# The last feed-forward layer in one written order, its last tile's cluster scores first, three tiles' bias on TensorE, and the last block's gate ahead of an out product

## The chip, the cores and the metric

One core of one Trainium2 chip (eight cores, of which the kernel uses one). The metric is device microseconds of one launch. A core has TensorE (PE; its weight loads are PEld), VectorE (DVE), ScalarE (ACT), GpSimd (POOL) and SyncE (SP), which issues most DMAs; each works through its own instructions in order, and engines wait for each other by semaphores.

## What is computed

Four residual layers over x, 4 sequences of 256 tokens with 512 channels, in f32:

```python
x = x + attention(layernorm(x))        # 32 heads, with an adapter prefix
x = x + ffn(layernorm(x))              # cluster-gated feed-forward
x = x + mixer(layernorm(x))            # state-space mixer: 8192 inner channels in 8 groups
x = x + ffn(layernorm(x))              # the same feed-forward weights again

def ffn(x):                            # x: 1024 tokens x 512
    dots = softmax(x @ centroids.T / 0.1)      # 64 clusters
    hits = dots > 0.01
    query_sel = any(hits, axis=1)              # a token is used if it hits any cluster
    cluster_sel = any(hits, axis=0)            # a cluster counts if any token hits it
    row_sel = cluster_sel[assignments]         # 512 outputs, each in a cluster
    return where(query_sel[:, None] & row_sel[None, :], x @ weight.T + bias, 0)

def mixer(x):
    proj = x @ in_proj_w.T             # gate (8192), xBC (conv of 4 taps, silu), dt
    y = ssd(...)                       # chunked scan with decays, + D * hs
    g = y * silu(gate)
    g = g / sqrt(mean of g*g over a group of 1024 channels + eps) * norm_w
    return g @ out_w.T
```

A column of `row_sel` depends on all tokens. So the last layer's result can be put into x only when the cluster scores of all tiles are there.

## The kernel before

**Tiles.** Tokens lie on the 128 partitions, in 8 tiles (TT = 8). The 512 channels are 4 pieces of 128 (KC = 4). Every f32 product is made of three matmuls on split operands, written by `mm3`: high x high (L115), high x low part of the weights (L116) and low x high (L117), for each of the pieces of the contraction. The high part is a rounding copy, made by ACT; the low part is a subtraction, made by DVE. Weights and activations are both split.

**Mixer.** The 8192 inner channels are 64 blocks of 128 (NB = 64), in 8 groups G of 8 (GB = 8). `block(i)` makes block i's x projection (24 matmuls `pp`), conv, the decays (`em`: ACT exponentials, DVE products) and the chunk products of block i-1 (`inner_products`, 64 matmuls `pyy`), and the gate projection of block i (24 matmuls `pp`, then ACT's silu, `gt`, in `gate`). `turn` transposes block i-1 (eight transposes `trx` in two PSUM tiles), `weigh` makes `xd` from them. Gated blocks `gb` are stored to DRAM (`spill`) and read again a token tile at a time (`recall`, tile `gr`, four blocks for one tile). Squares for the norm are summed in `sq` (`squared`), and summed over channels by `pqs` with `root` behind it.

**Out product.** `outer(q, t)` multiplies group q's `gh` (split `gr`) of token tile t with the split output weights `wo` into `pog`: two halves of 12 matmuls with 512 columns. It is done a group later, one tile in a block; `scaled` (L1237 on DVE) adds pog times the norm's factor to x. `upper_half` makes the high part (ACT, L1215) and leaves the low part (DVE, L1220) as a `lower` to be called later; `upper_out` does the same for output weights (L1174, L1177); `lowered()` calls all that are pending. The last group G-1 has no later group: its first halves are in `begin`/`begun`, and its second halves belong to the last feed-forward part. There the last of the eight pieces comes from a tile in SBUF (128 columns), and `gr` has only three pieces (384 columns). The chunk scores of the mixer (`scores`, matmuls `pg`, L1038, and DVE's `gm`, L1045) for the next group are made in the group's seventh block.

**Pools.** PSUM pool "m" has two slots, shared by `trx`, `pog` of `outer`, `pg`, `tr`; a matmul into it waits for the reader of the tile two before.

**Last feed-forward part.** For a tile: norm statistics (DVE, L138, L139), `root` (ACT Sqrt, L143), `scale` to gxn (DVE, L158), 4 transposes `tr` (PE), split into gxs (ACT L107, DVE L108), two halves of 12 matmuls with 288 columns into `pd` (64 cluster scores and 512 outputs together), then `chosen`: the row maximum (gnm), Exp on ACT (L218), hits, two bias adds (L229, L230) and one select-and-add (L231). After the last tile `select` counts hits over all tokens (cnt, msk), and eight times `take` (L243) copies the chosen columns into x, each with its output DMA.

**Order.** All blocks are under `manual_schedule`: the order on the engines is the program's. The last feed-forward part is not: a scheduler of the framework orders it, from costs and due times. ACT's Sqrt and Exp need different function tables, and a table load is put where the function changes.

Of the kernel before, what the change touches and what calls it, by code (L numbers as in the profile page):

```python
# [9 lines left out]
F32 = mybir.dt.float32  # L10
F32R = mybir.dt.float32r
# [3 lines left out]
AF = mybir.ActivationFunctionType  # L15
# [64 lines left out]
def hybrid_kernel(  # L80
# [29 lines left out]
    def mm3(o, ls, rs, first=True, last=True):  # L110

        n = len(ls)
        for k in range(n):
            (lh, ll), (rh, rl) = ls[k], rs[k]
            nc.tensor.matmul(o, lh, rh, start=(first and k == 0), stop=False)  # L115
            nc.tensor.matmul(o, lh, rl, start=False, stop=False)  # L116
            nc.tensor.matmul(o, ll, rh, start=False, stop=(last and k == n - 1))  # L117
# [57 lines left out]
    class Feed:  # L175


        def __init__(self, name, w1, p2):
            self.norm = Norm(name)
            self.name, self.p2 = name, p2  # L180
            t = lambda n, s, d=F32: w1.tile(s, d, name=f"{name}{n}")
            self.bias = t("b", [P, C])
            load(self.bias, ffb.to_broadcast([P, C]))
            idx = t("i", [NCL, 1])
            load(idx, cst[:NCL, COLS["idx"][0] : COLS["idx"][1]])
            asg_i = t("a", [NCL, C], I32)
            load(asg_i, asg.to_broadcast([NCL, C]))
            self.onehot = t("o", [NCL, C], BF16)
            nc.vector.tensor_scalar(self.onehot, asg_i, idx, None, ALU.is_equal)
            self.w = [t(f"w{j}", [P, KC, 2, FH], F32R) for j in range(2)]  # L190
            self.new = t("x", [P, TT, C])
            self.hits = t("h", [P, NCL])
            nc.gpsimd.memset(self.hits, 0.0)
# [9 lines left out]
                self.products(xs, j, halves[j])  # L203
            self.chosen(t, halves)

        def products(self, xs, j, o):
            mm3(o, [[v[:, k, :] for v in xs] for k in range(KC)],
                [[v[:, k, j, :] for v in self.w] for k in range(KC)])

        def chosen(self, t, halves):  # L210
            p2 = self.p2
            pa, pb = halves
            small = lambda n, w: p2.tile([P, w], F32, name=f"{self.name}{n}", tag=f"f{n}")
            nm = small("nm", 1)
            nc.vector.tensor_reduce(nm, pa[:, :NCL], AX.X, ALU.max, negate=True)
            nc.vector.tensor_scalar(nm, nm, 10.0, None, ALU.mult)
            e, se = small("e", NCL), small("se", 1)
            nc.scalar.activation(e, pa[:, :NCL], AF.Exp, bias=nm, scale=10.0, accum_out=se)  # L218
            nc.vector.reciprocal(se, se)
            hit, sel = small("hit", NCL), small("sel", 1)  # L220
            nc.vector.tensor_scalar(hit, e, se, 0.01, ALU.mult, ALU.is_gt)
            if t < TT - 1:
                nc.vector.tensor_tensor(self.hits, self.hits, hit, ALU.max)
            else:
                self.last = hit
            nc.vector.tensor_reduce(sel, hit, AX.X, ALU.max)
            new = self.new[:, t, :]
            m = FH - NCL
            nc.vector.tensor_tensor(new[:, :m], pa[:, NCL:], self.bias[:, :m], ALU.add)  # L229
            nc.vector.tensor_tensor(new[:, m:], pb, self.bias[:, m:], ALU.add)  # L230
            nc.vector.scalar_tensor_tensor(new, new, sel, x[:, t, :], ALU.mult, ALU.add)  # L231

        def select(self, cnt, rows):

# [551 lines left out]
    def mixer(feed, later):  # L786
        with ExitStack() as es, ExitStack() as inner:
# [504 lines left out]
                return q, t, po  # L1292

            xs2, gts, ems, xds, gbs = {}, {}, {}, {}, {}
            late_ = []

            def gate(i, pp):
                gts[i] = p2.tile([P, NT], F32, name="gt", tag="gt", bufs=2)
# [77 lines left out]
            def block(i):  # L1376
# [81 lines left out]
                        next(scoring)  # L1458

                next(g_steps)  # L1460
                if done or both:
                    inner_products(i - 1)
                    if both:
                        done = outer(G - 2, TT - 1)
                    pp = next(g_steps)
                    scored()
                    next(g_steps)
                else:
                    pp = next(g_steps)
                    scored()  # L1470
                    next(g_steps)
                    inner_products(i - 1)
                lower.append(upper_piece(n + 3))
                if g and gi == 0:
                    lower.append(upper_half(g - 1, 0))
# [5 lines left out]
                if both:  # L1481
                    for k in range(3):
                        fetch_out(NB - 3 + k)
                    begin(0)
                    lower.extend(upper_out(g * GB + k) for k in range(4))
                    scaled(*done)
                    lowered()
                    lower.extend(upper_out(g * GB + k) for k in range(5, GB))
                    begin(1)
                    lowered()  # L1490
                if scoring:
                    for _ in scoring:
                        pass
                if gi == 6:
                    for k in range(4):
                        fetch_out(g * GB + k)
# [7 lines left out]
                    group[NEXT[gi] + "pp"] = whole(projected(NEXT[gi], g + 1))  # L1504
                    upper_piece(n + 4)()

            pos, begins = {}, {}

            def begin(t):
                begins[t] = parts(G - 1, t, 0)  # L1510

            def begun(t):
                if t not in begins:
                    begin(t)
                pos[t] = ps_o.tile([P, C], F32, name="pog", tag="po")
                partial(pos[t], G - 1, begins.pop(t), 0)

            with tc.manual_schedule(
                engines={e.engine for e in (nc.tensor, nc.scalar, nc.vector, nc.gpsimd)}
            ):  # L1520
                opening()
                for i in range(2, NB):
                    block(i)
                es_p.close()
                ps_o = pool("m_o", 4, space=PSUM, **freed)
                i = NB - 1
                spilled(i - 1, gbs[i - 1])
                decays(i)
                turn(i)
                weigh(i)  # L1530
                begin(2)
                upper_out(i - 3)()
                wos[G - 1].insert(4, wos[G - 1].pop())
                for t in range(3):
                    begun(t)
                begin(3)
                squared(i - 1, xs2.pop(i - 1), gbs.pop(i - 1))
                inner_products(i)
                spilled(i, gbs[i])
                begun(3)  # L1540
                partial(pos[0], G - 1, parts(G - 1, 0, 1), 1)
                squared(i, xs2.pop(i), gbs.pop(i))
                rgs[G - 1] = root(sums(G - 1))
                nc.vector.reciprocal(rgs[G - 1], rgs[G - 1])
            es_y.close()
            inner.close()
            ps_d = pool("f_d", 2, space=PSUM, side="right", **freed)
            f1, f2 = pool("f1", 1, **freed), pool("f2", 2, **freed)
            feed = Feed("g", f1, f2)
            for k in range(KC):  # L1550
                feed.weights(k)
            ov = out.rearrange("(t p) c -> p t c", p=P)
            turned_ = {}

            def fed(t):
                where = (ps_o, "po") if t == TT - 1 else (ps_d, "pd")
                feed.tile(
                    t, turned_.pop(t), [where[0].tile([P, FH], F32, name="pd", tag=where[1]) for _ in range(2)]
                )

            for t in range(TT):
                po = pos.pop(t)
                if t:
                    partial(po, G - 1, parts(G - 1, t, 1), 1)
                scaled(G - 1, t, po)
                if t + 4 < TT:
                    begun(t + 4)
                feed.norm.stats(t)
                rooted = feed.norm.root(t, t + 1)

                with tc.issue_after(rooted) if t == TT - 1 else ExitStack():
                    for n in range(*{TT - 2: (0, 0), TT - 1: (t - 2, t)}.get(t, (max(0, t - 1), t))):
                        fed(n)
                xn = f2.tile([P, C], F32, name="gxn", tag="gxn")
                tr = ps.tile([P, KC, P], F32, name="tr", tag="m")
                turned_[t] = [f2.tile([P, KC, P], F32R, name=f"gxs{j}", tag=f"gxs{j}", bufs=3) for j in range(2)]
                feed.norm.turned(t, xn, tr, turned_[t])
            primed(AF.Exp)
            fed(TT - 1)
            feed.select(ps.tile([NCL, P], F32, name="cnt", tag="m"), ps.tile([P, C], F32, name="msk", tag="m"))  # L1580
            for t in range(TT):
                feed.take(t)
                load(ov[:, t, :], x[:, t, :])

    later = ExitStack()
    mixer(attention(later), later)
# [69 lines left out]
```

## Time and profile before

| | us |
|---|---|
| runs: median (lowest, highest), 3 runs | 1847.87 (1845.71, 1849.84) |
| the profiled execution: time | 1849.91 |
| its span, first to last instruction | 1848.1 |
| mean granted TensorE clock in the span | 0.986 |
| PE busy | 1777.1 |
| DVE busy | 1425.8 |
| ACT busy | 1276.9 |

The span runs from the first to the last instruction; the launch's time is 1.8 us longer than the span in this execution. Times in the text are us from the span's start. "Idle before" in a group's row is the time in which the engine did nothing before these instructions, with what ended it. The granted clock is 1.00 at full speed and 0.50 at half. In the part concerned: the last gate projection 1742.0 to 1747.4, the first products of the last group's tiles from 1748.4, pog(1,1) from 1774.6, first `pd` finished at 1787.1, last `pd` at 1837.0, takes 1838.9 to 1843.9, end 1848.1.

### The profile page before, as it was taken

The page shows a single profiled execution, that of the slowest core. Times are in us where ns is not written, and L with a number is a line of the kernel's source. Part 1 is how long each engine was busy: PE and PEld are TensorE (multiplying, and loading weights), DVE is VectorE, ACT ScalarE, POOL GpSimd, SP SyncE. Part 2 cuts the span into 40 slices and gives each one's busy share as a digit, 9 for nine tenths or more (in the row PEclk, how much of TensorE's full clock was granted, in tenths as well). Part 3 has the DMA queues.
Part 4 walks back from the last instruction along what each step waited for, and adds up shares of the span by engine and source line. Part 5 has one row for each costly group of instructions (what it writes and reads, how often), then busy time and mean ns, then how long its engine had stood idle before and what let it go on. Part 6 is the DMA issues. An engine that isn't in the chain of part 4 may idle for free.

```text
span 1848.1 us, 33082 instructions
## 1 busy us (share of the span) xinstructions
PE 1777.1 (96%) x12882; PEld 1448.5 (78%) x12882; DVE 1425.8 (77%) x2155; ACT 1276.9 (69%) x2520; POOL 245.0 (13%) x251
## 2 busy tenths in 40 slices
PE   7999989899999999999999999999999999999997
PEld 6777767677777888888888888888888888888776
DVE  5566667678989787878887787879787878887766
ACT  6666676367778667866776686668667866767743
POOL 6322330000110111001101110110111011101100
PEclk9999999999999999999999999999999999999999
DMA  4000000112325323432442343224333532343231
GB/s 146 1 1 1 23 15 2 47 59 86 103 86 160 107 95 111 140 104 92 125 135 78 106 162 99 98 86 160 92 104 97 160 104 92 110 137 114 92 88 50
DMA packets 134238, 169.45 MB, mean 92 GB/s; under 512 B 12225, under 2 KB 77377, under 8 KB 134081
## 3 DMA queue, kind: packets, MB, share of 16 engines
q1 hardware_dynamic: 125008, 134.30, 23.9%
q10 hardware_dynamic: 9072, 33.03, 4.7%
q8 instruction: 101, 1.65, 0.4%
q14 instruction: 57, 0.46, 0.1%
HBM read 131.64 MB, written 35.65 MB: 91 GB/s over the span
## 4 chain that ended last, share of the span: by engine, by line
PE 80%; DVE 8%; ACT 7%; issue 2%; POOL 2%; DMA 1%; SPq 0%; ACTq 0%; DVEq 0%; POOLq 0%
PE pp L115 13%; PE pp L116 13%; PE pp L117 13%; PE pyy L1120 7%; PE pog L115 6%; PE pog L117 6%; PE pog L116 6%; PE trx L1101 3%; ACT e L477 2%; PE ptr L493 1%; DVE acc L1008 1%; PE pq L115 1%; ACT em L1081 1%; PE pg L1038 1%; PE pq L116 1%
## 5 line engine op out<-in xcount | busy, mean ns | idle before, releaser
L115 PE MATMUL pp<-mx,w 128*128 128x512 f32 (+1 forms) x1160 | 463.6, 400 | 5.7 <-DVE acc L1008 5.1
L117 PE MATMUL pp<-mx,w 128*128 128x512 f32 (+1 forms) x1160 | 452.0, 390 | 0.0
L116 PE MATMUL pp<-mx,w 128*128 128x512 f32 (+1 forms) x1160 | 451.5, 389 | 0.0
L1153 POOL TENSOR_TENSOR sq<-sq,x 128x1024 f32<-128x1024 f32 x54 | 129.9, 2406 | 1205.0 <-ACT x L1152 1205.0
L115 PEld LDWEIGHTS pp<-mx,w 128*128 128x128 f32 x1160 | 218.3, 188 | 51.5 <-issue 5.5
L117 PEld LDWEIGHTS pp<-mx,w 128*128 128x128 f32 x1160 | 218.3, 188 | 46.3 <-DVE w L830 0.7
L116 PEld LDWEIGHTS pp<-mx,w 128*128 128x128 f32 x1160 | 218.7, 189 | 40.6
L1008 DVE SCALAR_TENSOR_TENSOR acc<-pp,cw_s,acc 128x1012 f32<-128x1012 f32 (+2 forms) x192 | 244.7, 1274 | 6.1 <-ACT acc L997 1.5
L1094 DVE TENSOR_TENSOR em<-em,gm 128x1280 f32<-128x1280 f32 x128 | 189.5, 1489 | 74.4 <-ACT em L1089 74.4
L115 PE MATMUL pog<-wo,gh 128*128 128x512 f32 x512 | 201.7, 394 | 3.4 <-ACT gh L1215 3.4
L117 PE MATMUL pog<-wo,gh 128*128 128x512 f32 x512 | 200.7, 392 | 1.0 <-DVE gh L1220 1.0
L116 PE MATMUL pog<-wo,gh 128*128 128x512 f32 x512 | 200.4, 391 | 0.0
L1104 DVE TENSOR_TENSOR xd<-trx,dt_t 128x512 f32<-128x512 f32 x128 | 82.4, 686 | 151.3 <-PE trx L1101 151.3
L1020 ACT ACT_TABLE_LOAD x63 | 80.8, 1283 | 154.6 <-DVE acc L1008 154.5
L1299 ACT ACTIVATE gt<-pp 128x1024 f32<-128x1024 f32 x64 | 65.6, 1026 | 156.5 <-PE pp L117 156.4
L1120 PEld LDWEIGHTS pyy<-em,xd 64*64 64x64 f32 x4096 | 129.5, 134 | 44.6 <-issue 18.4
L1081 ACT ACTIVATE em<-r,end_t 128x128 f32<-128x128 f32 x512 | 163.0, 389 | 0.8
L1120 PE MATMUL pyy<-em,xd 64*64 64x256 f32 (+3 forms) x4096 | 157.6, 302 | 2.4 <-DVE em L1094 2.4
L477 ACT ACTIVATE e<-sc,nmx 128x256 f32<-128x256 f32 (+1 forms) x256 | 104.2, 442 | 21.0 <-DVE nmx L471 20.9
L115 PEld LDWEIGHTS pog<-wo,gh 128*128 128x128 f32 x512 | 96.5, 189 | 23.6 <-ACT gh L1215 3.9
L117 PEld LDWEIGHTS pog<-wo,gh 128*128 128x128 f32 x512 | 96.6, 189 | 22.3 <-DVE gh L1220 2.2
L116 PEld LDWEIGHTS pog<-wo,gh 128*128 128x128 f32 x512 | 96.7, 189 | 19.5
(293 smaller groups left out, 3180.5 us busy)
## 6 DMA issues: line engine op xcount, KB each, us to landing
wr<-in_win_dram SPq DMA_DIRECT2D x144, 256.0 KB, 2.7
r<-cumd SPq DMA_DIRECT2D x256, 128.0 KB, 2.9
spill<-gb ACTq DMA_DIRECT2D x63, 512.0 KB, 3.2
gr<-spill SPq DMA_DIRECT2D x120, 256.0 KB, 3.5
wor<-in_wout_dram SPq DMA_DIRECT2D x64, 256.0 KB, 4.4
out_dram<-x SPq DMA_DIRECT2D x8, 256.0 KB, 2.5
x<-in_x_dram SPq DMA_DIRECT2D x1, 1536.0 KB, 8.8
gr<-spill SPq DMA_DIRECT2D x8, 192.0 KB, 2.5
```

The lines of the kernel that those rows point to most:

```text
L115: nc.tensor.matmul(o, lh, rh, start=(first and k == 0), stop=False)
L116: nc.tensor.matmul(o, lh, rl, start=False, stop=False)
L117: nc.tensor.matmul(o, ll, rh, start=False, stop=(last and k == n - 1))
L477: nc.scalar.activation(es_[c][:, 2 * j + pr, :], sc[:, j, :], AF.Exp, bias=nm[:, j : j + 1], accum_out=rs[:, c, h : h + 1],)
L1008: nc.vector.scalar_tensor_tensor(av[:, :, d:], pv[:, :, : L - d], cw_s[:, ch, tap : tap + 1], av[:, :, d:], ALU.mult, ALU.add,)
L1020: nc.scalar.activation(pair(x2).rearrange("p k u i -> p u k i"), acc.rearrange("p (u k i) -> p u k i", u=2, i=Q), AF.Silu,)
L1081: nc.scalar.activation(piece(e, j, c, 2 - c, 2), rv[:, j, 2:, :], AF.Exp, bias=end_t[:, 2 * j + c, h : h + 1],)
L1094: nc.vector.tensor_tensor(e, e, gm, ALU.mult)
L1104: nc.vector.tensor_tensor(xd[:, hs, :].rearrange("p c (h d) -> p c h d", h=2), tr.rearrange("p c (h d) -> p c h d", h=2), dt_t[:, hs, 2 * ...
L1120: nc.tensor.matmul(py[d, u, j * L + c * Q : (j + 1) * L].rearrange("p (k i) -> p k i", i=Q), xd[us, 4 * j + c, d], piece(es2[hh], j, c)[us ...
L1153: (nc.gpsimd if n < NB - 2 else nc.vector).tensor_tensor(sqs[g], sqs[g], x2, ALU.add)
L1299: nc.scalar.activation(gts[i], pp, AF.Silu)
```

## The change

1. In `Feed`, the bias tile gets 64 zero columns in front (a POOL memset in each of the two feed-forward layers), so that it lies as the products do. `products` can take a range of columns, and can begin its group with one plain f32 matmul of the identity with the bias. `chosen` becomes a generator, `choice`, with the hits before the outputs; where `biased`, the two bias adds and the select become two select-and-adds straight from PSUM. The last layer does this for tiles 5, 6 and 7.
2. In block 63, the gate projection goes ahead of `inner_products(62)` and of out product (6, 7). The recalls, output-weight pieces and lowers around them are in a new order, with `scaled` behind the pending lowers, and the output-weight pieces 5 to 7 after the decays.
3. In block 6 of group 0 the steps 1 and 2 of the next group's `scores` go after both halves of the gate, and the other two wait for block 7.
4. The last feed-forward part comes under `manual_schedule`, in a written order: in a loop for t = 2 to 6, second half of pog(t), x(t), statistics, recall and high parts for t+3 and t+1, root, Exp table, transposes of t-1, products and choice of t-2, Sqrt table, the lowers that are left, and the first half of pog(t+3). `primed(...)` loads a table ahead by an activation of one column.
5. At the end, tile 7's 64 cluster columns are computed before its other columns, the count and mask before its second half, and seven takes before tile 7's select.

The order on ACT in one turn of the loop before and after the change is different: after it, root, Exp table load, gxs, Exp, Sqrt table load, then the high parts of the next turn. On DVE the lower of gh(t+1,1) stands behind `choice(t-2)` for t = 2, 3, 4.

```diff
@@ Feed
-            self.bias = t("b", [P, C])
+            self.bias0 = t("b", [P, NCL + C])
+            self.bias = self.bias0[:, NCL:]
+            nc.gpsimd.memset(self.bias0[:, :NCL], 0.0)
...
-        def products(self, xs, j, o):
-            mm3(o, [[v[:, k, :] for v in xs] for k in range(KC)],
-                [[v[:, k, j, :] for v in self.w] for k in range(KC)])
+        def products(self, xs, j, o, cols=slice(0, FH), biased=False):
+            if biased:
+                nc.tensor.matmul(
+                    o[:, cols], ident, self.bias0[:, FH * j + cols.start : FH * j + cols.stop],
+                    start=True, stop=False,
+                )
+            mm3(o[:, cols], [[v[:, k, :] for v in xs] for k in range(KC)],
+                [[v[:, k, j, cols] for v in self.w] for k in range(KC)], not biased)
...
-            nc.vector.tensor_tensor(new[:, :m], pa[:, NCL:], self.bias[:, :m], ALU.add)
-            nc.vector.tensor_tensor(new[:, m:], pb, self.bias[:, m:], ALU.add)
-            nc.vector.scalar_tensor_tensor(new, new, sel, x[:, t, :], ALU.mult, ALU.add)
+            for part, cs in ((pa[:, NCL:], slice(0, m)), (pb, slice(m, C))):
+                if biased:
+                    nc.vector.scalar_tensor_tensor(
+                        new[:, cs], part, sel, x[:, t, cs], ALU.mult, ALU.add
+                    )
+                else:
+                    nc.vector.tensor_tensor(new[:, cs], part, self.bias[:, cs], ALU.add)
+                yield
+            if not biased:
+                nc.vector.scalar_tensor_tensor(new, new, sel, x[:, t, :], ALU.mult, ALU.add)
...
@@ block
                 next(g_steps)
-                if done or both:
+                for _ in pending:
+                    for _ in pending.pop():
+                        pass
+                if done and not both:
                     inner_products(i - 1)
-                    if both:
-                        done = outer(G - 2, TT - 1)
                     pp = next(g_steps)
                     scored()
                     next(g_steps)
                 else:
                     pp = next(g_steps)
+                    next(g_steps)
                     scored()
-                    next(g_steps)
                     inner_products(i - 1)
+                if both:
+                    done = outer(G - 2, TT - 1)
...
                 if both:
...
-                    begin(0)
+                    lower.append(made(0, 0))
                     lower.extend(upper_out(g * GB + k) for k in range(4))
+                    lower.append(made(1, 0))
+                    lowered()
                     scaled(*done)
-                    lowered()
-                    lower.extend(upper_out(g * GB + k) for k in range(5, GB))
-                    begin(1)
-                    lowered()
-                if scoring:
+                if scoring and g:
                     for _ in scoring:
                         pass
+                elif scoring:
+                    pending.append(scoring)
...
@@ after the blocks
                 decays(i)
                 turn(i)
                 weigh(i)
-                begin(2)
-                upper_out(i - 3)()
+                multiplied(0, 0)
+                multiplied(1, 0)
+                lower = [upper_out(i + k - 7) for k in (5, 6, 7)]
+                lower.append(made(2, 0))
+                lower.append(upper_out(i - 3))
...
+                settled(0)
+                normal(0)
+                multiplied(1, 1)
+                lower = made(4, 0)
+                settled(1)
+                lower()
+                multiplied(4, 0)
+                normal(1)
...
+                for t in range(2, TT - 1):
+                    multiplied(t, 1)
+                    settled(t)
+                    lower = [made(t + 3, 0)] if t + 3 < TT else []
+                    lower.append(made(t + 1, 1))
+                    lower.pop(0)()
+                    normal(t)
+                    lower.append(turned_(t - 1))
+                    for j in range(2):
+                        product_half(t - 2, j)
+                    lower.pop()()
+                    for _ in choice(t - 2):
+                        pass
+                    primed(AF.Sqrt)
+                    for f in lower:
+                        f()
+                    if t + 3 < TT:
+                        multiplied(t + 3, 0)
...
+                product_half(t, 0, slice(NCL, FH))
+                feed.select(cnt, ps.tile([P, C], F32, name="msk", tag="m"))
+                product_half(t, 1)
+                for _ in c6:
+                    pass
+                for t in range(TT - 1):
+                    feed.take(t)
+                    load(ov[:, t, :], x[:, t, :])
+                for _ in c7:
+                    pass
+                feed.take(TT - 1)
+                load(ov[:, TT - 1, :], x[:, TT - 1, :])
```

Here `made(t, half)` recalls gh(t, half), makes its high part and returns its lower; `multiplied(t, half)` is the 12 matmuls of that half of pog(t); `settled(t)` is `scaled` and the statistics; `normal(t)` is root, the Exp table and gxn; `turned_(t)` is the transposes and the high part of gxs, and returns its lower; `product_half(t, j, cols)` is half j of `pd`.

## The prediction

> **What bounds the kernel now.** I read the busy shares and the chain first, then the windows of the last 114 us, TensorE's waits there, and last the groups that give durations.
>
> ```profile
> PE 1777.1 (96%) x12882; PEld 1448.5 (78%) x12882; DVE 1425.8 (77%) x2155; ACT 1276.9 (69%) x2520; POOL 245.0 (13%) x251
> PE 80%; DVE 8%; ACT 7%; issue 2%; POOL 2%; DMA 1%; SPq 0%; ACTq 0%; DVEq 0%; POOLq 0%
> ```
>
> TensorE is the bound nearly everywhere: an order can only remove its few holes, or make new ones. The windows of the end (span start to 1848.1; busy us of PE, PEld, DVE, ACT, POOL, then clock, DMA share, GB/s):
>
> ```profile
> 1742.00:1748.00 6.00, 6.00 (x30) 4.97 (x29) 6.00 (x11) 3.59 (x7) 0.15 (x1) 1.00 0.33 100
> 1754.00:1757.00 3.00, 0.96 (x3) 0.40 (x2) 1.83 (x2) 2.97 (x7) 0.00 (x0) 0.89 0.00 0
> 1757.00:1765.00 8.00, 7.50 (x75) 5.25 (x74) 3.15 (x5) 2.35 (x4) 0.00 (x0) 0.62 0.63 176
> 1804.00:1814.00 10.00, 10.00 (x64) 9.16 (x64) 7.59 (x25) 6.43 (x13) 0.00 (x0) 1.00 0.00 1
> 1825.00:1831.00 6.00, 4.64 (x34) 4.07 (x33) 4.60 (x16) 3.48 (x8) 0.00 (x0) 1.00 0.00 0
> 1837.00:1848.00 11.00, 1.30 (x6) 0.47 (x5) 6.83 (x15) 0.00 (x0) 0.00 (x0) 0.71 0.52 191
> ```
>
> Two holes: 2.0 us in 1754 to 1757 (2.2 from end to start in the timeline) with half clock behind it (0.62, and in the timeline from 1756.3 to 1763.15), and 1.8 us at 1828 to 1830. The feed-forward loop between (1804 to 1814) is dense: a tile's first product starts 9.28 us after the last one's (1787.29, 1796.54, 1805.82).
>
> ```profile
> PE pog L115 <- ACT gh L1215: 3.4, 2, 2.0
> PE tr L166 <- DVE gxn L158: 1.2, 1, 1.2
> PE pog L117 <- DVE gh L1220: 1.0, 2, 0.5
> ```
>
> The durations that I use (mean ns after "busy us"):
>
> ```profile
> L231 DVE SCALAR_TENSOR_TENSOR gx<-gx,gsel,x 128x512 f32<-128x512 f32 x8 | 6.0, 746 | 0.1
> L108 DVE TENSOR_TENSOR gxs<-tr,gxs 128x512 fp32r<-128x512 f32 x7 | 4.8, 687 | 2.9 <-ACT gxs L107 2.9
> L230 DVE TENSOR_TENSOR gx<-pd,gb 128x288 f32<-128x288 f32 x8 | 3.6, 456 | 4.5 <-PE pd L117 4.5
> L229 DVE TENSOR_TENSOR gx<-pd,gb 128x224 f32<-128x224 f32 x8 | 3.0, 372 | 0.0
> L1220 DVE TENSOR_TENSOR gh<-gr,gh 128x384 fp32r<-128x384 f32 x5 | 2.7, 548 | 1.2 <-PE pd L117 1.2
> L218 ACT ACT_TABLE_LOAD x6 | 7.7, 1283 | 2.4 <-DVE gnm L216 2.3
> ```
>
> In the timeline, successive matmuls start 0.227 us apart for 512 columns (12 of a half tile: 2.73) and 0.1325 for 288 (24 of `pd`: 3.18); a tile's 4 transposes take 0.44. So a feed tile's TensorE work is 2 x 2.73 + 3.18 + 0.44 = 9.07 of the 9.28.
>
> **A. Blocks 6 and 7 of group 0 (scores later): -1.0.** Before, `pg` waits 1.6 us and block 7's `trx` 1.7 us for DVE's gm (waits, 510 to 545). With steps 3 and 4 in block 7 both go. But block 7's `gb` is also held by ACT's exponentials and DVE's products, which start only 0.95 earlier: gain 1.0, ends 0 and 2.7.
>
> **B. Block 63 to the start of pog(1,1): -5.1.** The gate's 24 matmuls go ahead of `pyy`(62) and of the 24 of pog(6,7); nothing is saved in work, but ACT's gate can start at 1746.2 (it waited until 1747.85 before) and the exponentials (5.34 us from table load to last) end with it. New order on PE from 1734.27: gate 5.45, pyy(62) 2.34 and pog(6,7) 5.45 to 1747.51, first four transposes 0.44. Then a new wait: block 63's second four need a PSUM slot that is freed by DVE's `scaled` (L1237), and this now stands behind three gb operations 2.58, four differences 1.87, a gh lower 0.60, four output-weight lowers 2.64, another lower 0.60: from 1742.2 DVE reaches and ends it at 1751.2. PE stalls 3.3 us. After that pog(0,0) and (1,0) to 1757.14, when DVE's second weigh (1755.44) is past: pyy(63) starts at once where it waited before, to 1759.48 at full clock; three more pog (8.18) to 1767.66 and pqs 1.84 to 1769.5. Before it was 1774.62.
>
> **C. Clock: +2.0.** The row for 1757 to 1765 shows what a hole costs here: 2.2 us of idle, then 6.8 us at half clock. The 3.3-us stall is longer, so I expect the same: half clock for about 3.4 us at least, hence +1.7, up to 3.4 if a second stretch follows[...]. [...] I keep +2.0 (ends 0 and 3.4).
>
> **D. First feed-forward part: +4.8.** ACT now has a written order: root(0), the Exp table load with its priming, and only then the hi cast of gh(4,0). From pqs at 1769.5: root 0.35, reciprocal 0.2, x(0), statistics, aggregate 1.6, root 0.3, load and priming 1.5: the cast starts at 1774.0 and ends at 1774.55. PE has done pog(1,1) at 1772.2 and stalls 2.4, then 0.3 for the lower. pog(2,1) then waits for its cast behind Sqrt load, root(1), Exp load and two casts of the feed weights (0.85), and for the DVE lower (1.55). Together 5.1 of stalls; before had about 0.3 of that stretch. SP's loads move too: the recall of gr(1,1) goes ahead of the bias and weight loads, gr(4,0) and gr(2,1) come between weights. They land in 2.5 to 3.6 us, ahead of their casts, so I cost the queue at nothing; if that cover went, a landing would be added to D. POOL's memset of the 64 columns is one more like the 0.15-us one of `hits`; POOL is idle there: nothing.
>
> **E. Loop t = 2, 3, 4: +4.6.** The lower part of gh(t+1,1) (L1220, 128x384) now stands on DVE behind all of `choice(t-2)`, and pog(t+1,1)'s third matmul needs it. So a ring closes, from one such lower to the next: the rest of pog(t,1) 2.4; x, statistics, aggregate 1.6; root 0.31; Exp load 1.3 and priming 0.2; gxs hi on ACT 0.6 and lower on DVE 0.62; the two gnm 0.40; exponential 0.55; reciprocal, ghit, hits, gsel 0.65; two bias adds and L231 1.45; the lower 0.55; some 0.2 of hand-overs. Sum 10.8, against 9.28: +1.5 per tile, three times. Before, the scheduler had the lower ahead of these. DVE is busy only some 7.0 of the 10.8: it is not throughput but order. [...] In the trace an exponential starts 1.30 us after its load started (1811.70, 1813.00)[...].
>
> **F. t = 5 to the end: +2.8.** For tiles 5, 6, 7 the two bias adds (0.46 + 0.37 per tile) leave DVE; a plain-f32 identity matmul enters PE six times. No row has one of this size: `pa` (L421, plain f32, 256 columns) takes 0.427 each in pitch[...], so 288 columns are an estimated 0.48 and 224 0.37: 5 x 0.48 + 0.37 = 2.77. Ends: 0.8[...] and 3.3. Tile 7's 64 columns by themselves: 12 at no less than 0.11 (the one-column steps of pqs) plus 12 x 224 columns at some 0.105, against 12 x 0.1325: +1.0 (ends 0.3 and 1.5). pog(7,1) stands behind pd(4), so x(7) comes at 15.9 us after the start of pog(5,1), not 13.3, and its transposes stall 1.6. Against it tile 7's other columns (1.6 + 1.6) go behind the count. Counted: cnt 26.6 after that start (before 25.2), msk 27.7, first take 28.65, seven takes to 32.9, tile 7's select and take to 34.75, then the output's 4.2 (as from 1843.86 to 1848.1): 39.0 against 36.24.
>
> **Sum.** -1.0 - 5.1 + 2.0 + 4.8 + 4.6 + 2.8 = +8.1. The profiled execution took 1849.91 (span 1848.1 and 1.8 around it), 2.0 over the median. So the span would be 1856.2, and against the median 1847.87 + 8.1 = **1856.0**.
>
> **Rivals.** (1) The forecast, about 0.56: the order closes the ring of E and the stalls of D. (2) More half clock, 0.18: [...] two or three more stretches of 1.7 to 3.4: about 1862. (3) No change, 0.14: D is half of what I count (ACT gets to gh(4,0) before its priming matters) and E +2: 1847.9 - 1 - 5.1 + 2 + 2.4 + 2 + 2 = 1850. (4) Faster, 0.12, by one mechanism: the lower of gh(t+1,1) lands before its matmul. TensorE reaches that at 9.1 + 0.43 after pog(t,1)'s start; if it is there, the ring never binds. It needs DVE and ACT to do the tile 1.5 us faster than my row-by-row sum, in D as well as E, from which A and B stay whole: 1847.9 - 6.1 + 0 to 1 of F = about 1842. For it: DVE and ACT have 20 to 30% idle in the loop. Against: the idle is waits for each other, in a chain. (5) Also under (3) and (4): that the change doesn't do what its words say. The bias on TensorE loads the engine that is the bound; it helps only where DVE is last. The row of L230 shows DVE idle for 4.5 us before those adds, for TensorE's `pd`: there it is TensorE that is last.
>
> **How the numbers follow.** The measurement can tell about 0.2% (3.7 us) from no change: 1844.2 to 1851.6. Faster is case 4, 0.12; same is case 3, 0.14; slower is cases 1 and 2, 0.74. The range runs from 1848.5, leaving out case 4 and a little of case 3, to 1863.5, leaving out the upper third of case 2: with the unknown ends of C and F (+1.4 and +1, or -2 and -2.7) inside.
>
> **What would show it.** Right: PE idle of about 3 us on `trx` of block 63 with DVE's `scaled` (x, L1237 as of before) as releaser; clock under 1 shortly behind it; pyy(63) without a wait; PE waits for ACT gh (2.4) and three times 1.3 to 1.9 for DVE gh of 128x384; starts of pog(t,1) 10.6 to 11 us apart; pd from gb at 0.45 to 0.5 each; last take some 4 us before the end. Wrong: starts still 9.3 apart (E), no ACT gh wait (D), no hole at trx (B, C), or the time from pog(5,1) to the end at or under 36.

## The result, and the profile after

The changed kernel takes 1855.95 us (median of 6 runs, 1851.77 to 1857.8) against 1848.86 (6 runs); the ratio is 1.0039, with a 95% interval of 1.0023 to 1.0056. It is slower, by about 7.1 us; forecast were 1856.0 and +8.1.

The page's busy line and the shares of its chain, for the kernel after (span 1855.7):

```profile
PE 1780.4 (96%) x12906; PEld 1452.3 (78%) x12906; DVE 1426.9 (77%) x2152; ACT 1286.0 (69%) x2536; POOL 245.3 (13%) x253
PE 78%; DVE 9%; ACT 8%; issue 2%; POOL 1%; DMA 1%; SPq 0%; ACTq 0%; DVEq 0%; POOLq 0%
```

TensorE's busy time is up by 3.3 us and the span by 7.6. So more than half of the loss is idle time of TensorE, and in the chain PE has 78% of the span where it had 80%, and DVE and ACT have 1% more each. The waits of TensorE from 1734 us on say where (line, releaser, us in total, times, longest):

```profile
PE pog L117 <- DVE gh L1245: 6.0, 5, 2.1
PE trx L1126 <- DVE x L1262: 3.1, 1, 3.1
PE pog L115 <- ACT gh L1240: 2.8, 2, 2.0
PE tr L1610 <- DVE gxn L158: 1.2, 1, 1.2
PE msk L264 <- DVE gc L263: 0.4, 1, 0.4
```

In the mixer the lines of after are 25 higher than those of before; L1245 is the gh lower, L1262 is `scaled`. Before, the DVE gh wait was 1.0 and there was no `trx` wait. The windows of the end (columns as above):

```profile
1748.00:1754.00 6.00, 2.94 (x15) 2.52 (x16) 5.85 (x9) 5.92 (x16) 0.15 (x1) 1.00 0.44 131
1754.00:1757.00 3.00, 3.00 (x15) 2.30 (x13) 3.00 (x4) 3.00 (x6) 0.00 (x0) 1.00 0.02 5
1757.00:1765.00 8.00, 8.00 (x89) 6.60 (x89) 7.40 (x11) 3.82 (x8) 0.00 (x0) 1.00 0.43 136
1794.00:1804.00 10.00, 9.57 (x48) 8.09 (x46) 6.25 (x18) 5.38 (x11) 0.00 (x0) 0.83 0.14 43
1814.00:1825.00 11.00, 9.52 (x57) 8.48 (x58) 6.45 (x19) 4.70 (x10) 0.00 (x0) 1.00 0.06 18
```

The hole is at 1748 to 1754 now (2.94 of 6.00 busy), and the row for 1757 to 1765, which had 0.62 before, is at full clock: the 3.1-us stall brought no half clock in this execution. A stretch at 0.83 turns up in the feed-forward loop instead.

Stages between the same instructions compare the executions better than times from the start. Block 4's silu starts anywhere from 481.0 to 488.7 us in the eleven profiles, though all that the change puts ahead of it is a memset on POOL, while the stretch from block 20's silu to block 61's takes 884.04 or 884.05 in every one. From starts in the timelines:

| stage | forecast | before | after | change |
|---|---|---|---|---|
| A: silu of block 4 to silu of block 9 | -1.0 | 89.53 | 88.62 | -0.9 |
| B: silu of block 61 to pog(1,1) | -5.1 | 71.81 | 66.89 | -4.9 |
| C: half clock behind the `trx` stall | +2.0 | (in B) | none | 0 |
| D: pog(1,1) to the second tile's transposes, less the pd that lies in it before | +4.8 | 9.33 | 14.02 | +4.7 |
| E: three turns of the loop (before: 3 x 9.28) | +4.6 | 27.84 | 34.44 | +6.6 |
| F: the rest of the span | +2.8 | | | +1.5 |

With 0.7 from the part ahead of block 4 these make the 7.6 of the span, to rounding. In A the waits of 1.6 and 1.7 us for DVE's gm are gone; TensorE's waits between 510 and 560 us sum to 2.8 instead of 4.4.

The ring of E, in the timeline of after (start, us, engine, line, operation; one turn, from statistics to lower):

```profile
1797.78 0.30 ACT L143 ACTIVATE grs<-gmv,eps 128x1 f32<-128x1 f32 x1 [1.91 <-DVE gmv L139]
1798.09 1.28 ACT L127 ACT_TABLE_LOAD   x1
1799.39 0.20 ACT L127 ACTIVATE primed<-ones 128x1 f32<-128x1 f32 x1
1799.50 0.57 ACT L1611 CAST gxs<-tr 128x512 fp32r<-128x512 f32 x1
1800.10 0.69 DVE L1612 TENSOR_TENSOR gxs<-tr,gxs 128x512 fp32r<-128x512 f32 x1 [0.92 <-ACT gxs L1611]
1801.20 0.32 ACT L233 ACTIVATE ge<-pd,gnm 128x64 f32<-128x64 f32 x1 [1.14 <-DVE gnm L231]
...
1801.65 0.16 DVE L235 RECIPROCAL gse<-gse 128x1 f32<-128x1 f32 x1 [0.54 <-ACT ge L233]
1803.19 0.75 DVE L255 SCALAR_TENSOR_TENSOR gx<-gx,gsel,x 128x512 f32<-128x512 f32 x1
1803.86 0.55 DVE L1245 TENSOR_TENSOR gh<-gr,gh 128x384 fp32r<-128x384 f32 x1
...
1804.46 0.50 PE L117 MATMUL pog<-wo,gh 128*128 128x512 f32 x1 [0.89 <-DVE gh L1245]
```

Each engine waits for another in turn. The lower ends at 1804.41, and at 1804.46 TensorE starts the third matmul of pog(4,1), which closes the ring. The starts of that matmul are 11.5, 11.9 and 11.0 us apart.

### The profile page after: what moved, and what is told of

Its sections match the earlier page's. It is cut to its first block, busy times and chain, and to the rows that moved or that the text cites. A ratio compares the mean times of both kernels' runs of the same rounds, so it can differ in the third digit from the quotient of the medians.

```text
span 1855.7 us, 33140 instructions
## 1 busy us (share of the span) xinstructions
PE 1780.4 (96%) x12906; PEld 1452.3 (78%) x12906; DVE 1426.9 (77%) x2152; ACT 1286.0 (69%) x2536; POOL 245.3 (13%) x253
## 4 chain that ended last, share of the span: by engine, by line
PE 78%; DVE 9%; ACT 8%; issue 2%; POOL 1%; DMA 1%; SPq 0%; ACTq 0%; DVEq 0%; POOLq 0%
PE pp L115 13%; PE pp L116 12%; PE pp L117 12%; PE pyy L1145 7%; PE pog L117 6%; PE pog L115 6%; PE pog L116 6%; PE trx L1126 3%; ACT e L502 2%; DVE acc L1033 1%; PE ptr L518 1%; PE pq L115 1%; ACT em L1106 1%; PE pg L1063 1%; PE pq L116 1%
```

## The experiments

**1. The lower out of the ring.**

```diff
@@ loop for t, kernel after
                     lower.pop(0)()
                     normal(t)
-                    lower.append(turned_(t - 1))
+                    for f in lower:
+                        f()
+                    lower = turned_(t - 1)
...
-                    for f in lower:
-                        f()
```

> The kernel after, with one edit: in the loop for t = 2 to 6 the lower of gh(t+1,1) stands on DVE right behind gxn(t), ahead of gxs and of choice(t-2). Theory (ring through choice): starts of the tiles' products fall from 11.0-11.9 us apart to about 9.3, the three DVE gh waits inside the loop (1.5 to 2.1 us each) vanish, and the time falls by 5 to 6.5 us, to about 1850 (ratio to before about 1.000). Rival (DVE or ACT throughput sets the pace, not order): starts stay 10.5 or more apart, the waits move to another releaser, under 1.5 us gained.

Measured: 1849.53 us (14 runs), ratio to before 1.0004 (0.9994 to 1.0014). The turns take 9.08 us each, TensorE's own work and nothing else. The window of three turns:

```profile
1784.00:1811.00 27.00, 27.00 (x156) 23.96 (x155) 19.97 (x54) 16.45 (x33) 0.00 (x0) 1.00 0.17 49
```

27.00 of 27.00 us busy, with DVE at 74%. One place in DVE's order was worth 6.4 us in the medians; throughput was not the bound of the loop.

**2. `scaled` ahead of the lowers in block 63.**

```diff
-                    lowered()
                     scaled(*done)
+                    lowered()
```

> The kernel after, with one edit: in block 63 DVE's scaled of out product (6,7) stands ahead of the pending lowers instead of behind them. Theory (the second four transposes wait for this instruction): their stall falls from 3.1 to about 0.9 us; but pyy(63) then waits for the decays' products at about 1755.5, so only 1.5 to 2 of the 2.2 reach pog(1,1), and the time falls by about 1.7 us. Rival (ACT's exponentials or the lowers themselves bind): the stall moves to pog(0,0) or to pyy(63) whole, and pog(1,1) starts within 0.5 us of where it did (1769.5).

Measured: 1855.79 us, as after (ratio to before 1.0037, 1.0023 to 1.0051). TensorE's waits, those that changed:

```profile
PE pog L117 <- DVE gh L1245: 7.0, 6, 2.2
PE pyy L1145 <- DVE em L1119: 0.5, 1, 0.5
PE trx L1126 <- DVE x L1262: 0.4, 1, 0.4
PE pog L116 <- DVE wo L1202: 0.4, 1, 0.4
```

The stall at `trx` fell from 3.1 to 0.4, more than I expected. But of these 2.7 us pog(0,0) lost 0.7 behind the lowers, pyy(63) 1.1 behind the decays and the products after it 0.5: from block 61's silu to pqs it is 64.78 us against 65.19. My 1.7 was wrong and the rival right, that the stall moves on. The window of this stretch:

```profile
1749.00:1758.00 9.00, 7.84 (x36) 5.45 (x34) 8.58 (x12) 8.92 (x20) 0.15 (x1) 1.00 0.29 89
```

DVE and ACT are both busy nearly throughout (8.58 and 8.92 of 9.00 us). Which of the two binds was not tried apart.

**3. The bias of tiles 5 to 7 back on DVE.**

```diff
-                BIASED = (5, 6, 7)
+                BIASED = ()
```

> The kernel after, with the bias of tiles 5, 6 and 7 added on DVE again, none by TensorE. Theory (the bias matmuls cost TensorE about 0.4 to 0.48 each on the path that sets the end; DVE has room before the count): the count comes 1.5 to 2.4 us earlier, but DVE's select of tiles 6 and 7 costs 0.6 more each behind it, so 0.5 to 1.5 us are gained. Rival (what the change was made for: DVE binds at the end): DVE's 1.9 us more are on the path, and the time rises by 1 to 2 us.

Measured: 1857.64 us, ratio to before 1.0051 (1.0035 to 1.0068), an interval that overlaps with that of after: unclear. In its profile the transposes of tile 7 wait 2.2 us instead of 1.2, for without bias matmuls TensorE arrives earlier; behind them TensorE runs at half clock, and from those transposes to the count it takes 9.82 us instead of 8.08. Half clock stands behind the `trx` stall too, where after has none. So this run could not tell the bias from the clock, and I repeated it without the ring (7).

**4. The blocks' part alone, the tail as before.** The blocks are those of after up to the square of block 63; from there on stands the text of before.

```diff
@@ kernel after, from the last squared() on
-                lower = made(1, 1)
...
-                settled(0)
-                normal(0)
...
+            for t in range(TT):
+                po = pos.pop(t)
+                if t:
+                    partial(po, G - 1, parts(G - 1, t, 1), 1)
+                scaled(G - 1, t, po)
+                if t + 4 < TT:
+                    begun(t + 4)
...
```

> The change's blocks alone (scores of group 0 later, gate of block 63 first, its lowers and the first products of the last group in the new order), with the last feed-forward part left to the scheduler as before, bias on DVE. Theory (the front is a gain of 5, which the written order of the tail gives back): pog(1,1) starts about 5 us earlier than before (1769.5 against 1774.6), the tail's 73 us are as before, and the time falls by 4 to 5 us to about 1844 (ratio 0.997 to 0.998). Rival (the front's gain is taken up by the tail's first waits, whatever its order: casts of recalled tiles and weights come no earlier): pog(1,1) starts earlier, but the first pd block and the end do not, under 1.5 us gained.

Measured: 1843.52 us (20 runs), ratio to before 0.9977 (0.9969 to 0.9985): 4.9 us faster in the medians, and faster than both kernels. Waits from 1730 us on:

```profile
PE trx L1126 <- DVE x L1262: 3.1, 1, 3.1
PE tr L166 <- DVE gxn L158: 1.0, 1, 1.0
PE pog L115 <- DVE x L1262: 0.4, 1, 0.4
PE msk L264 <- DVE gc L263: 0.4, 1, 0.4
```

None is of gh: with the scheduler's order the tail takes the front's gain to the end. So the tail of after (its order, its bias matmuls and the split of tile 7 together) costs what the front gives, and 7 more.

**5. Casts ahead of root and table, 6. no Exp priming before the loop.**

```diff
@@ on top of experiment 1
                 settled(0)
+                made(4, 0)()
                 normal(0)
                 multiplied(1, 1)
-                lower = made(4, 0)
+                lower = made(2, 1)
                 settled(1)
                 lower()
...
-                lower = made(2, 1)
                 turned_(0)()
-                lower()
@@ experiment 6, besides
-                    primed(AF.Exp)
+                    if t > 1:
+                        primed(AF.Exp)
```

> The kernel with the early lower (e1_lower_early), and in the first feed-forward part the recall of gh(4,0), its high part and its lower ahead of root(0), those of gh(2,1) ahead of the second tile's statistics and of the feed weights' casts. Theory (the 5 us of stalls before the loop come from ACT's written order: root and Exp table load ahead of a cast): the ACT gh wait of 2.0 us and the DVE gh waits of 1.4 us go, and from pog(1,1)'s start to the second tile's transposes it takes 9.5 to 10.5 us instead of 14.0; the time falls by 3.5 to 4.3 from e1's 1849.5, to about 1845.5. Rival (the recalls' DMAs or the feed weights land no earlier): PE waits for gr by way of ACT gh at another place, or the first pd block waits for gw; under 1.5 us gained.

> e5_casts_first without the Exp priming of tiles 0 and 1, which no Exp uses: two Exp and two Sqrt loads of 1.28 us less on ACT before the loop. Theory: after e5 ACT has still 5 us of useless loads there, ahead of the feed weights' casts; if pd(0) waits for those in e5, it starts earlier and 0.5 to 2 us more are gained; if it doesn't, nothing. [...]

Measured: 5 takes 1850.48 us, ratio 1.0014 (1.0001 to 1.0027), no gain on experiment 1; 6 takes 1848.67, ratio 0.9991 (0.9979 to 1.0004). In 5 the waits for ACT gh are gone, as expected, but others came:

```profile
PE pd L115 <- ACT gw L107: 1.4, 1, 1.4
PE pog L117 <- DVE gh L1245: 0.8, 1, 0.8
PE pd L117 <- DVE gxs L1612: 0.5, 1, 0.5
PE pd L116 <- DVE gw L108: 0.4, 1, 0.4
```

The first `pd` now waits for the feed weights' cast on ACT: the rival's second form. From pqs to the fifth tile's transposes it is 43.76 us in the profile, 0.8 more than the 42.96 of experiment 1, though TensorE waits 1.0 less in it (3.1 against 4.1): 3.4 us of half clock stand behind the new hole. Without the four useless table loads (6) it is 40.01. The casts of the last two feed-weight pieces on ACT, in 5 and then in 6:

```profile
1777.20 1.38 ACT L107 CAST gw<-gr 128x576 fp32r<-128x576 f32 x2 [2.57 <-DMA gr<-in_ffw_dram]
1784.09 1.39 ACT L107 CAST gw<-gr 128x576 fp32r<-128x576 f32 x2 [2.75 <-DMA gr<-in_ffw_dram]
```

They wait for a DMA in both. SP issues these loads 0.2 to 0.3 us behind the casts of the first two pieces, whose two buffers they take, and in 5 those casts stand behind the table loads: without the loads the second casts start 12.1 us after pqs instead of 14.8. TensorE's waits in this stretch fall from 3.1 to 1.2, and the half clock, which 6 does not have there, can have cost up to 1.7 (an estimate: half of 3.4). That is nearly all of the 3.75 us between 5 and 6. So of D's 4.7 us, 3.0 came back with the order and the loads together; the order alone gained nothing, with a half-clock stretch on top of it. What a load itself costs on ACT is in the timeline above: it takes 1.28 us, and the next activation starts 1.30 us after the load's start in the kernel after (1798.09, 1799.39), and 1.29 to 1.30 behind 160 of its 164 loads.

From the 1855.95 of after, experiments 1, 5 and 6 get back 7.3 us. Experiment 4 stays 5.2 us below 6 in the medians; from pqs to the end the profiles have 75.00 us in 4 and 77.81 in 6. What makes this rest was not followed further.

**7. The bias once more, where nothing else binds.** Experiment 6 with `BIASED = ()`.

> e6_no_early_exp with the bias of tiles 5, 6, 7 on DVE: the comparison of e3 once more, where no ring holds the loop. Theory (on the path the bias matmuls cost TensorE about 1.3 between tile 7's transposes and the count, and save DVE about 1.1 behind the count): the same time as e6 within 0.8 us as long as the clock is full behind tile 7's transposes. Rival (DVE binds at the end, the change's bias is a gain): slower than e6 by 1.5 us or more at full clock too. In between or with a half-clock stretch behind those transposes: the bias matmuls only keep TensorE busy enough there.

Measured: 1847.79 us (21 runs), ratio 0.9996 (0.9987 to 1.0005), against 0.9991 (0.9979 to 1.0004): the same. Behind the loop the profiles differ at one place. With the bias on DVE (7) the windows ahead of, in and behind a stretch that follows tile 7's transposes, and then, with the bias on TensorE (6), the same stretch:

```profile
1817.00:1822.00 5.00, 2.80 (x23) 2.60 (x22) 4.31 (x11) 2.68 (x7) 0.00 (x0) 1.00 0.00 0
1822.00:1829.00 7.00, 7.00 (x34) 7.00 (x33) 4.23 (x17) 1.65 (x7) 0.00 (x0) 0.53 0.00 0
1829.00:1832.00 3.00, 2.62 (x20) 2.04 (x18) 0.70 (x4) 0.00 (x0) 0.00 (x0) 0.95 0.00 0
```

```profile
1829.00:1836.00 7.00, 5.78 (x44) 5.36 (x43) 5.66 (x23) 3.47 (x10) 0.00 (x0) 1.00 0.00 0
```

7 loses 1.74 us from these transposes to the count, at half clock, and 1.05 behind it on DVE, but arrives at the transposes no later. In both profiles without the bias matmuls the half clock stands there, and in none of the five that have them with this written tail. Yet the median of 7 is 0.9 us lower than that of 6 and its ratio 0.0005 higher, both inside the spread: so the bias neither gained nor lost anything that the runs can tell, and whether its use is to keep TensorE busy there stays open.

**8. The gate ahead, and nothing else.** On the kernel before:

```diff
-                if done or both:
+                if done and not both:
                     inner_products(i - 1)
-                    if both:
-                        done = outer(G - 2, TT - 1)
...
                     inner_products(i - 1)
+                if both:
+                    done = outer(G - 2, TT - 1)
```

> The kernel before with one edit: in block 63 the gate's 24 matmuls go ahead of inner products (62) and out product (6,7); lowers, recalls and output-weight pieces stay in the order of before, scores and tail too. Theory (the front's gain needs ACT's order as well: three more output-weight casts still stand ahead of the gate on ACT and wait for out product (6,7)): the exponentials start no earlier than about 1748.9, the hole ahead of the last blocks' products stays about 2 us, and from block 61's silu to pqs it takes 67 to 69 us (before 68.65, the front of e4_front_only 65.2); the time is within 1.5 us of before. Rival (the gate's move is the gain by itself): 65 to 66 us, and 3 to 4 us faster than before.

Measured: 1849.52 us (14 runs), ratio 1.0007 (0.9999 to 1.0015). Waits and the window of the hole:

```profile
PE pog L115 <- ACT gh L1215: 3.1, 2, 1.7
PE pog L117 <- DVE gh L1220: 1.6, 2, 1.1
```

```profile
1754.00:1757.00 3.00, 0.76 (x3) 0.33 (x3) 3.00 (x4) 3.00 (x5) 0.00 (x0) 0.98 0.01 3
1757.00:1765.00 8.00, 8.00 (x81) 6.29 (x82) 3.81 (x6) 1.27 (x3) 0.00 (x0) 0.80 0.64 180
```

The same hole as before the change, and half clock behind it again: 3.4 us here and 3.4 more from 1773.9, where the kernel before had one stretch of 6.8. From block 61's silu to pqs it is 68.41 us (before 68.65). The gate's move by itself gives nothing. So what the blocks gain beyond A's 0.9 needs what stands around the gate in the new order: ACT's casts of three output-weight pieces leave the place ahead of the gate's silu (43.4 us behind block 61's silu in after, 1746.00 less 1702.57; 45.5 here, 1746.78 less 1701.31), and block 63's products (`pyy`) come ahead of pog(2,0), whose cast stands behind the exponentials on ACT. These two were not tried apart, nor without the gate's move.

Nor is B's gain all order. The 6.8 us of half clock of the kernel before (1756.3 to 1763.2) lie in B, and after has none there. The 12 matmuls and the 64 that run in them take about 3 us more than at full clock (an estimate: 6.2 and 2.7 us from start to start, against 3.4, with a wait of 0.5 in it, and 2.3). So up to 3 of B's 4.9 are clock in this pair of profiles. How often the kernel before has that stretch no run here shows.

**9. Experiment 4 with `scaled` first.**

> The kernel with the new blocks and the old tail (e4_front_only), with scaled of out product (6,7) ahead of the lowers as in e2_scaled_first. Theory: full-clock time is 0.4 us shorter, as in e2, and the 3.1-us stall that brought half clock in two of the seven profiles goes, some 2 us each time: on average about 1 us faster than e4, 1842.5, which the runs can hardly tell. Rival: the lowers, now later, put a wait of the same length into pog(0,0) and the half clock stays; no gain or a loss of up to 1 us.

Measured: 1843.22 us (14 runs), ratio 0.9973 (0.9963 to 0.9982), against 0.9977 (0.9969 to 0.9985) for 4: it can't be told from it. 64.77 us from block 61's silu to pqs against 65.18, as in experiment 2. These two beat both kernels.

## Why the prediction was right, and where its sum was lucky

**Right, and shown.** A (-0.9 for -1.0) and B (-4.9 for -5.1, with the `trx` stall at 3.1 for 3.3 and `scaled` as its releaser) stand in the stages, and experiment 4 has 4.9 of their 5.8 as time. D is +4.7 for +4.8 with both of its waits, which the profile puts at 4.1 us together where 5.1 had been counted. Experiment 5 shows that ACT's written order makes the first, and 5 and 6 that more than a third of D can't be had back so simply, for the feed weights are late next. Their landing was the cover that I had named; what put it off were the table loads ahead of the first casts. The mechanism of E was tested by removing one thing: experiment 1 brought the turns from 11 or more to 9.08 us. The rival of a faster chain fell with the timeline of after: the ring closed.

**Mis-sized terms.** E was put at 10.8 us per turn and measured 11.05 undisturbed, 0.75 for three; the first turn held 0.5 us more (in the timeline a feed-weight lower stands ahead of x(2) on DVE, which I had left out); and about 0.8 is a half-clock stretch within the second. So +6.6 for +4.6.

F was put at +2.8 and is 1.5, but three readings in it were wrong, and they cancel in part. First, it sets 39.0 us from the start of pog(5,1) against 36.24 before, and these do not hold the same work. Before, tile 3's products (pd) end just ahead of pog(5,1):

```profile
1812.05 0.29 PE L117 MATMUL pd<-gw,gxs 128*128 128x288 f32 x1
1812.18 0.40 PE L115 MATMUL pog<-wo,gh 128*128 128x512 f32 x1
```

After, they come behind it and lie in the 39.0. From 1812.18 to the end it is 35.9, and with these 3.2 us the base is 39.1: on its own rows F was about zero. Second, the count, put at 26.6 us, comes at 29.3 (counted from 1815.2, where pog(5,1) would start without its stall: the next transposes at 1817.9 less the 2.7 of its 12 matmuls): 1.8 of this are the 224 other columns of tile 7's first half with their bias, which stand ahead of the count, and the working had them behind it. Third, "then the output's 4.2": before, eight output DMAs follow eight takes 0.61 us apart, at up to 414 GB/s, and from the last take to the end it is 4.26; after, one DMA stands behind the last take and it is 3.14. The split of tile 7 cost 1.1 for 1.0.

The bias matmuls took 0.47 each (two halves of a tile with bias start 2.06 us apart, 12 matmuls 1.59), for 0.48 forecast, but that was luck: the matmuls of `pa` are not plain f32 but on the rounded operands that the split products use (F32R in the code). They leave one record each, 0.116 us apart at full clock and 0.213 at half, and 0.427 is two of the latter. The bias matmuls do leave two records each (12 for six at L210 in after).

**The step that failed: C.** I put half clock behind the 3.1-us stall with certainty enough to add 2.0. In the profile of after it did not come; it came in the loop instead. Of the seven profiles that have this stall, five kept the full clock behind it and two (3 and 6) did not; from block 61's silu to pqs they took 1.6 and 2.8 us longer. What goes with it can be read from the traces. In each of the eleven profiles all half-clock stretches start whole multiples of 3.413 us apart (in after the one at 1794.04 is 359 of them behind the one at 568.66), and up to TensorE's last products each lasts one, two or three of them (in the kernel before, seven of 3.41 us and three of 6.83). Their starts lay a grid of 3.413 us over an execution. The steps of it that the stall touches, in after, and in experiments 3 and 6 the step that holds it and the stretch behind:

```profile
1746.26:1749.67 3.41, 1.73 (x10) 1.24 (x8) 3.41 (x7) 3.38 (x7) 0.00 (x0) 1.00 0.62 210
1749.67:1753.09 3.42, 2.03 (x11) 1.77 (x12) 3.27 (x6) 3.39 (x9) 0.15 (x1) 1.00 0.40 121
```

```profile
1744.18:1747.59 3.41, 0.34 (x4) 0.10 (x3) 3.41 (x7) 3.37 (x9) 0.00 (x0) 1.00 0.47 154
1747.59:1751.00 3.41, 3.41 (x11) 2.83 (x12) 2.83 (x4) 3.38 (x9) 0.15 (x1) 0.50 0.28 82
```

```profile
1748.21:1751.62 3.41, 1.24 (x8) 0.83 (x6) 3.41 (x6) 3.38 (x8) 0.00 (x0) 1.00 0.60 192
1751.62:1758.45 6.83, 5.93 (x16) 4.88 (x17) 6.22 (x9) 6.59 (x15) 0.15 (x1) 0.50 0.15 43
```

It is the same stall with the same instructions before it. Where two steps share it, the emptier one is busy for 0.48 to 0.51 of its time, in all five profiles with full clock; where one step holds most of it, 0.10 (3) and 0.36 (6), half clock follows. Among the steps at full clock from 1735 us on that end ahead of the last matmul, every one busy for 0.43 or less was followed by half clock in the eleven profiles, and of the fuller ones only one (0.61, experiment 8, at 1770.5). The part ahead of block 4 takes up to 7.7 us more in one profile than in another (481.0 to 488.7); that this is what moves the stall over the grid is my reading and was not shown. With these profiles the size of C (1.6 and 2.8) was right and its chance was not: 2 in 7 where I took it for nearly certain, so some 0.6 on average (an estimate from the two sizes and the seven profiles). The length of a stall alone does not tell either: this one is 3.1 us in all seven; those of 2.0 to 2.2 in the kernel before, in the loop of after and at tile 7's transposes (3 and 7) are shorter and had half clock behind them; the 2.0 us ahead of pog(4,0) in after had none.

So 1856.0 against 1855.95 is nearer than the terms were: C's 2.0 that weren't there and F's 1.3 too many stood against E's 2.0 too few, and the runs before shifted by 1.0. The mechanisms of A, B, D and E stand; that the sum met the median within 0.1 is luck.

**Rivals.** "No change" and "faster" had the tail's stalls half covered or gone; they were there. "More half clock" happens, but not at every hole: behind the `trx` stall it stood in two of seven profiles, and in after it stood in the loop instead.

## What to carry to other kernels

Where a fixed order is written for several engines, follow one turn of the loop across them: an instruction that feeds the bound engine should stand on its queue at the first place where its inputs are there, not behind work that itself waits for the turn (here one lower, 6.4 us). Moving work of the bound engine gained nothing by itself here; look at which instruction of another engine is released by it and what stands ahead of that one (experiments 4 and 8). When two parts of a change have opposite signs, run each alone: here the half that gained 4.9 us hid behind the half that lost 12. And before a hole is charged with half clock, look at several executions: here the same stall had it in two profiles of seven, a chance and not a fixed cost.

## What the runs showed of the hardware

- Half-clock stretches lie on a grid of 3.413 us in each execution, to within 0.01 us in eleven profiles. The same 3.1-us stall was followed by full clock in five profiles, where TensorE was busy for 0.48 to 0.51 of the emptier grid step that it touches, and by half clock for 3.4 and 6.8 us in two, where it was busy for 0.10 and 0.36.
- The same instructions at the start of the kernel, up to block 4, took between 481.0 and 488.7 us in the profiles, while the 884 us from block 20 to block 61 agreed within 0.01. The length of the start goes with the half clock in it: 23.9 us in the two shortest (7 and 9), 41.0 and 44.4 in the two longest (2 and 6).
- The spread of the runs of one kernel (5 to 13 us here) goes with the clock too: in experiment 5 the seven runs with a mean granted clock of 0.987 or more took 1844.55 to 1848.63 us, the seven with less 1852.32 to 1857.48.
